# Three expert steps in one loop: the 32-row code moved in front of the 64-row code

## The chip, the cores and the metric

The kernel runs on one core of one Trainium2 chip. The metric is the device time of one execution in microseconds (us); lower is better. The engines are named as the profile names them: PE (matrix multiply, with PEld for its weight loads), DVE (vector), ACT (scalar), POOL (GpSimd), SP (the engine that issues most DMAs). Each engine has a sequencer of its own that reads the engine's instructions, takes its branches and waits on its semaphores.

## The reference

The program normalizes 625 node vectors of 768 numbers, runs a two-layer graph attention network over 20000 edges, adds the result to the input, and then runs a transformer block of 12 attention heads whose feed-forward part is a top-1 mixture of 8 experts. Only that last part bears on this change. Cut to it:

```python
h2 = _ln(x, ln2_g, ln2_b).reshape(-1, d)              # 625 rows of 768
w, sel = jax.lax.top_k(h2 @ Wg, 1)                    # one expert for each row
hid = jax.nn.relu(jnp.einsum('nd,edf->enf', h2, W1) + b1[:, None, :])   # 768 -> 3072
y = jnp.einsum('enf,efd->end', hid, W2) + b2[:, None, :]                # 3072 -> 768
moe = jnp.einsum('ne,end->nd', combine, y)            # each row takes its own expert's y
return x + moe.reshape(b, t, d)
```

W1 and W2 of one expert are 9.4 MB each, in f32.

## The kernel before

Everything ahead of the experts is one straight line of code on every engine (but for one branch at L449 that is there for unusual edge lists). It ends about 700 us into the profiled execution.

**Routing.** The rows are scattered to memory in the order of their experts (`xg` for the layer's input, `xr` for the running sum with the row's number). The expert that the first 125 rows choose most is taken first: one block of 128 of its rows runs ahead of the loop, as straight-line code (`step_a`, L1179). What is left is cut by small vector operations (L1228 to L1306) into blocks of 128, 64 and 32 rows. `table` holds for each block its expert, whether that expert is new, its kind (0 for 128 rows, 1 for 64, 2 for 32) and its first row; `nblk` is their number. Within an expert the order is 32, 64, then all of 128 rows.

**The loop** (L1333) takes one block in each iteration. At its head every engine loads the kind from `table` (L1336), and POOL loads the rows of the next block and the sums of this one. Then one of three versions of the same step runs, chosen by nested conditions on the kind: in memory the code of each engine lies as it is written, the loop's head, the 128-row code, the 64-row code, the 32-row code, the loop's end. The end has the jump back to the head (L1333). A condition that fails is a jump over the code that is not taken; the branch records at L1346 and L1349 are these jumps, and also the jumps from the end of the 128-row and of the 64-row code to the loop's end.

**One step** (`step`, L1075) on M rows: `into(c)` multiplies the rows (`xbT`, turned beforehand) with a piece of W1 into PSUM `ph` (L1091), DVE copies it to `hb` (L1095); `turn(c)` transposes it on PE (`tph`, L1102), and ACT adds the bias and applies the relu into `hbT` (L1107); `out_of(c)` multiplies with a piece of W2 and adds up in PSUM `py` (L1114). Between the last pieces PE turns the rows of the next block (`tpx`, L891). DVE then adds `py` to the sums (`yo`, L1166), and POOL scatters them to the output (L1168). The order of PE's instructions within a step is written out by hand; the three versions do the same work with another split (M=64 and M=32 use groups of the array's columns).

**Weights.** The six pieces of an expert's weights (`ew`, three of W1 and three of W2) have one buffer each. `load_expert` (L1066) issues on SP, within the iteration, the loads of the next block's expert, in twelve DMAs of 1.5 MB and one for `b2b`; each waits until PE has read the piece that it overwrites, and is left out on the chip where the next block's expert is not new.

**Places in PE's code.** Counted from the hint at the loop's head as instruction 0, the built program of before has the first condition at 4, the 128-row code from 6 to 439, the second condition at 441, the 64-row code from 443 to 853, the 32-row code from 855 to 1395, and the jump back to the head at 1399.

Of the kernel before, what the change touches and what calls it, by code (L numbers as in the profile page):

```python
# [62 lines left out]
def gnn_moe_kernel(ctx: ExitStack, tc: tile.TileContext, p, out):  # L63
# [83 lines left out]
    with tc.tile_pool(name="gnn", bufs=1) as gp:  # L147
# [31 lines left out]
        with tc.tile_pool(name="oneh", bufs=12) as op_, \  # L179
# [48 lines left out]
            def step(at, on_act):  # L228
                o = op_.tile([R, SH + 1], F16, name="step")
                if on_act:  # L230
                    nc.scalar.activation(o, iota[:, :SH + 1], AF.Sign, bias=at, scale=-1.0)  # L231
                else:
                    nc.vector.tensor_scalar(o, iota[:, :SH + 1], at, 2.0, op0=OP.is_lt, op1=OP.mult)
                return o
# [821 lines left out]
    def sums_so_far(row):  # L1056
        rb = mw.tile([B, D + 1], F32, name="rb", bufs=1)
        nc.gpsimd.dma_start(rb, xr[ds(row, B), :])
        return rb

    def biases(e):
        bT = mw.tile([128, NK], F32, name="bT")
        of_e = bT_all.rearrange("p (e k) -> p e k", k=NK)[:, ds(e, 1), :]
        return bT, nc.vector.tensor_copy(bT, of_e.rearrange("p o k -> p (o k)"))

    def load_expert(e, new):  # L1066

        with tc.manual_schedule(engines={SP}):
            for l in range(2):
                for c in range(NFC):  # L1070
                    load_piece(e, l, c, cond=new)
                if not l:
                    load_bias(e, cond=new)
# [104 lines left out]
    bT, _ = biases(first_a)  # L1178
# [135 lines left out]
    xbT = ewb.tile([128, KD, B], F32, name="xbT")  # L1314
    row_0 = nc.values_load(table[0:1, 3, 0:1], engines=[pool], min_val=0, max_val=NR - B)
    first_rows = nc.gpsimd.dma_start(xb, xg[ds(row_0, B), :])
    first_turned, = step_a

    def next_expert(i):
        return (nc.values_load(table[0:1, 0, ds(i, 1)], engines=[SP], min_val=0, max_val=E - 1),  # L1320
                nc.values_load(table[0:1, 1, ds(i, 1)], engines=[SP], min_val=0, max_val=1))
# [3 lines left out]
    def all_of(step, e, new):  # L1325
        with tc.manual_schedule(engines={PE}):
            for _ in step:
                pass
        load_expert(e, new)
# [3 lines left out]
    with tc.For_i(0, n_blk, 1, iteration_sync="reg_based") as i:  # L1333
        e = nc.values_load(table[0:1, 0, ds(i, 1)], engines=[mybir.EngineType.DVE], min_val=0,
                           max_val=E - 1)
        kind = nc.values_load(table[0:1, 2, ds(i, 1)], min_val=0, max_val=2)  # L1336
        row, row_next = (nc.values_load(table[0:1, 3, ds(k, 1)], engines=[pool], min_val=0,
                                        max_val=NR - B) for k in (i, i + 1))

        nc.gpsimd.dma_start(xb, xg[ds(row_next, B), :])  # L1340
        rb = sums_so_far(row)
        bT, s = biases(e)
        tc.add_manual_dep(s.ins, first_rows.ins.name, ORDER)

        then = next_expert(i + 1)
        with tc.If(kind == 0) as cmp:  # L1346
            all_of(step(B, xbT, bT, rb, first_turned), *then)
        with cmp.Else():
            with tc.If(kind == 1) as cmp2:  # L1349
                all_of(step(64, xbT, bT, rb, first_turned), *then)  # L1350
            with cmp2.Else():
                all_of(step(32, xbT, bT, rb, first_turned), *then)


# [29 lines left out]
```

## Time and profile before

| | us |
|---|---|
| median of 3 runs (lowest, highest) | 1070.74 (1069.84, 1071.74) |
| the profiled execution's own time | 1070.6 |
| its span, from the first to the last instruction | 1067.9 |
| PE busy in the span | 1006.7 (94%) |
| the loop, first to last matmul | 700.1 to 1055.2 |

The nine iterations in the profiled execution, numbered from 0, by the first matmul of each:

| iteration | 0 | 1 | 2 | 3 | 4 | 5 | 6 | 7 | 8 |
|---|---|---|---|---|---|---|---|---|---|
| rows | 64 | 128 | 64 | 32 | 128 | 64 | 32 | 64 | 32 |
| starts at, us | 700.13 | 736.35 | 801.68 | 840.54 | 866.12 | 931.47 | 965.72 | 993.27 | 1027.52 |

In a line of the timeline, the columns are the start, the time taken, the engine, the line of code, the operation, what it writes and reads, the shapes, how many, and in brackets the idle time before and what ended it. Granted clock is the share of full speed that PE's clock had. The DMA view counts packets by queue; queues of the kind "instruction" bring code to the engines' sequencers.

### The profile page before, as it was taken

To read this page: it belongs to the slowest core of one execution; us is meant where nothing else is said; L and a number is where in the kernel's file an instruction comes from. 1 tells how busy PE (TensorE), PEld (TensorE's weight loads), DVE (VectorE), ACT (ScalarE), POOL (GpSimd) and SP (SyncE) were. 2 spreads that over 40 slices of the span, in tenths; PEclk is the share of its full clock that TensorE was granted. 3 is DMA by queue.
4 is the path that set the end of the run, shared out by engine and by line. 5 is a ranking of instruction groups with operands and counts; after the bars stand their busy time and mean duration, and the time that the engine had idled before them with its cause. 6 is when DMAs were issued, how large, how long until landed. Compare 5 with 4: busy or idle time off the path is not lost. (4 is left out here: it accounts for less than half of the span.)

```text
span 1067.9 us, 14435 instructions
## 1 busy us (share of the span) xinstructions
PE 1006.7 (94%) x4763; PEld 574.8 (54%) x4764; DVE 451.7 (42%) x1264; ACT 319.0 (30%) x817; POOL 57.1 (5%) x97
## 2 busy tenths in 40 slices
PE   6889999999999999999999999999999889998993
PEld 4455465677656556666665654544453435533341
DVE  6886786484284910665438544011101121011211
ACT  6677553452231111444435211110202112021120
POOL 1200100000000100000001101000000000000000
PEclk9999999999999999999999999999999899998997
DMA  9300500301300347998002679012799948899693
GB/s 286 129 1 1 181 9 0 133 1 43 93 14 0 103 120 220 398 389 293 1 2 63 237 251 351 12 46 58 304 321 387 408 177 322 294 413 409 248 412 153
DMA packets 85669, 194.48 MB, mean 182 GB/s; under 512 B 32397, under 2 KB 34068, under 8 KB 85609
## 3 DMA queue, kind: packets, MB, share of 16 engines
q1 hardware_dynamic: 79817, 174.00, 44.3%
q0 software_dynamic: 5712, 19.54, 5.3%
q8 instruction: 36, 0.59, 0.2%
q10 hardware_dynamic: 80, 0.16, 0.1%
q14 instruction: 24, 0.20, 0.1%
HBM read 251.98 MB, written 38.37 MB: 272 GB/s over the span
## 5 line engine op out<-in xcount | busy, mean ns | idle before, releaser
L1114 PE MATMUL py<-ew,hbT 128*64 128x384 f32 (+2 forms) x960 | 196.0, 517 | 12.8 <-DMA ew<-in_L_ffn_W_dram 12.8
L1091 PE MATMUL ph<-ew,xbT 128*32 128x256 f32 (+2 forms) x864 | 153.9, 499 | 7.8 <-issue 4.5
L1114 PEld LDWEIGHTS py<-ew,hbT 128*64 128x64 f32 (+2 forms) x960 | 91.6, 149 | 97.7 <-issue 62.3
L1107 ACT ACTIVATE hbT<-tph,bT 128x64 f32<-128x64 f32 (+2 forms) x240 | 55.3, 333 | 264.2 <-PE tph L1102 162.3
L1091 PEld LDWEIGHTS ph<-ew,xbT 128*32 128x32 f32 (+2 forms) x864 | 63.9, 135 | 87.2 <-issue 79.9
L1166 DVE TENSOR_TENSOR yo<-yo,py 64x384 f32<-64x384 f32 (+2 forms) x40 | 23.0, 608 | 182.9 <-PE py L1114 182.5
L1095 DVE COPY hb<-ph 128x512 f32<-128x512 f32 (+1 forms) x39 | 24.5, 629 | 149.8 <-PE ph L1091 149.8
L528 PE MATMUL agg<-xl,zT 125*125 125x256 f32 (+1 forms) x300 | 79.8, 417 | 1.3 <-ACT zT L517 1.1
L528 PEld LDWEIGHTS agg<-xl,zT 125*125 125x125 f32 x300 | 54.5, 188 | 19.6 <-ACT zT L517 2.6
L231 ACT ACTIVATE step<-iota,past 125x314 f16<-125x314 f16 x120 | 55.9, 548 | 0.0
L356 PE MATMUL pp<-w,yT 128*125 128x512 f32 x120 | 55.3, 600 | 0.0
L628 PE MATMUL ph<-wr,h1T 128*125 128x384 f32 x160 | 52.8, 486 | 0.0
L590 PE MATMUL ph<-w,h1T 128*125 128x384 f32 x160 | 52.4, 486 | 0.0
L837 ACT ACTIVATE e<-e,nm 125x125 f32<-125x125 f32 (+4 forms) x60 | 36.0, 602 | 39.5 <-DVE nm L834 39.5
L248 PE MATMUL cps<-step,oh 125*125 125x314 f16 x181 | 37.4, 309 | 10.5 <-ACT step L231 5.4
L900 PE MATMUL po<-wpj,aT 128*125 128x384 f32 x120 | 44.3, 499 | 1.2 <-DVE nm L834 0.7
L241 DVE TENSOR_SCALAR oh<-iota,drel,upper 125x125 f16<-125x125 f16 x160 | 41.2, 317 | 3.4 <-PE cps L248 3.4
L166 PE MATMUL ph<-wr,yT 128*125 128x512 f32 x96 | 42.1, 593 | 0.1
L590 PEld LDWEIGHTS ph<-w,h1T 128*125 128x125 f32 x160 | 30.0, 188 | 21.2 <-issue 0.5
L628 PEld LDWEIGHTS ph<-wr,h1T 128*125 128x125 f32 x160 | 29.8, 187 | 20.8
L808 PE MATMUL pq<-hT,L_ffn_Wq 128*128 128x313 f32 (+1 forms) x144 | 40.9, 432 | 0.0
L834 DVE CUSTOM_DVE_ANT_0 e<-sc,later 125x125 f32<-125x125 f32 (+4 forms) x60 | 30.7, 544 | 24.1 <-PE sc L828 23.9
(328 smaller groups left out, 1248.9 us busy)
## 6 DMA issues: line engine op xcount, KB each, us to landing
ew<-in_L_ffn_W_dram SPq DMA_DIRECT2D x132, 1536.0 KB
xr<-zt SPq DMA_DIRECT2D x5, 3076.0 KB
xg<-zt SPq DMA_DIRECT2D x5, 3072.0 KB
w<-in_L_gnn_W_dram SPq DMA_DIRECT2D x4, 1536.0 KB
wr<-in_L_gnn_Wr_dram SPq DMA_DIRECT2D x4, 1536.0 KB
b2b<-in_L_ffn_b_dram SPq DMA_DIRECT2D x11, 384.0 KB
xb<-xg POOLq DMA_DIRECT2D x10, 384.0 KB, 6.1
rb<-xr POOLq DMA_DIRECT2D x9, 384.5 KB, 7.0
```

What stands on the lines that cost most here:

```text
L166: nc.tensor.matmul(pp[:R, :], yT[:, c, cols(t)], part(wr1, KD, c, i, 512), start=(c == 0), stop=(c == KD - 1))
L231: nc.scalar.activation(o, iota[:, :SH + 1], AF.Sign, bias=at, scale=-1.0)
L241: m = nc.vector.tensor_scalar(o, iota[:, :n], at, weight, op0=OP.is_equal, op1=OP.mult)
L356: nc.tensor.matmul(pp[:R, :], yT[:, c, cols(t)], part(w1, KD, c, i, 512), start=(c == 0), stop=(c == KD - 1))
L528: nc.tensor.matmul(self.agg[:R, c0:c0 + n], zT[:, s, :], xl[:, s, x0:x0 + n], start=(s == 0), stop=(s == T - 1))
L590: nc.tensor.matmul(ph[:R, :384], h1T[:, c, cols(t)], part(w2, KH, c, i, 384), start=(c == 0), stop=(c == KH - 1))
L628: nc.tensor.matmul(ph[:R, :384], h1T[:, k, cols(t)], part(wr2, KH, k, i, 384), start=(k == 0), stop=(k == KH - 1))
L808: nc.tensor.matmul(pp[:, :b - a], w[:, c, c0:c0 + 128], hT[:, c, a:b], start=(c == 0), stop=(c == KD - 1))
L900: mm = nc.tensor.matmul(pp[:R, i, :384], aT[:, c, cols(t)], wpj[i][:, c, :], start=(c == 0), stop=(c == KD - 1))
L1091: mm = nc.tensor.matmul(ph[g * M:(g + 1) * M, :C], xT[:, k, :M], w[:, k, o + g * C:o + (g + 1) * C], start=(k == 0), stop=(k == KD - 1))
L1107: nc.scalar.activation(hbT[c][:, k, r], tp[:, k, r], AF.Relu, bias=bT[:, f:f + 1])
L1114: mm = nc.tensor.matmul(py[g * M:(g + 1) * M, i, :384], hbT[c][:, k, g * M:(g + 1) * M], w[:, o + g * K + k, i * 384:(i + 1) * 384], start ...
```

## The change

The two versions inside the `Else` change places in memory: the condition is now on kind 2 instead of kind 1, the 32-row code comes first, and the 64-row code last. No instruction of a step changes, and nothing within a step changes its place.

```diff
         then = next_expert(i + 1)
+
         with tc.If(kind == 0) as cmp:
             all_of(step(B, xbT, bT, rb, first_turned), *then)
         with cmp.Else():
-            with tc.If(kind == 1) as cmp2:
+            with tc.If(kind == 2) as cmp2:
+                all_of(step(32, xbT, bT, rb, first_turned), *then)
+            with cmp2.Else():
                 all_of(step(64, xbT, bT, rb, first_turned), *then)
-            with cmp2.Else():
-                all_of(step(32, xbT, bT, rb, first_turned), *then)
```

In PE's code the 32-row code now lies from 443 to 984 and the 64-row code from 986 to 1395; the head, the 128-row code and the loop's end stay where they were. A 64-row step now takes two jumps to its code and none to the loop's end; a 32-row step takes one jump to its code and one to the loop's end. The lines of code below the change are one higher than before (L1346 is L1347, L1349 is L1350).

## The prediction, made before the changed kernel ran

> **What bounds the kernel now.** I read the page first: PE is busy for 94% of the span, so time is lost only where PE waits. The change touches nothing ahead of 700 us, so I then took PE's timeline of the loop, shape by shape, and looked for idle time where iterations meet. Nine iterations meet eight times; only two of these meetings have a gap that no weight load explains.
>
> ```profile
> 729.07 5.38 PE L1114 MATMUL py<-ew,hbT 128*64 128x384 f32 x32
> 736.35 10.54 PE L1091 MATMUL ph<-ew,xbT 128*128 128x512 f32 x24 [1.90 <-DVE yo L1166]
> ...
> 830.61 5.38 PE L1114 MATMUL py<-ew,hbT 128*64 128x384 f32 x32
> 840.54 7.58 PE L1091 MATMUL ph<-ew,xbT 128*32 128x256 f32 x96 [4.55 <-issue]
> ...
> 858.13 0.84 PE L1114 MATMUL py<-ew,hbT 128*32 128x384 f32 x4
> 861.72 4.47 PE L1114 MATMUL py<-ew,hbT 128*32 128x384 f32 x28 [2.75 <-DMA ew<-in_L_ffn_W_dram]
> 866.12 10.57 PE L1091 MATMUL ph<-ew,xbT 128*128 128x512 f32 x24
> ...
> 960.41 5.38 PE L1114 MATMUL py<-ew,hbT 128*64 128x384 f32 x32
> 965.72 5.39 PE L1091 MATMUL ph<-ew,xbT 128*32 128x256 f32 x96
> ...
> 990.56 2.77 PE L1114 MATMUL py<-ew,hbT 128*32 128x384 f32 x28 [1.26 <-DMA ew<-in_L_ffn_W_dram]
> ```
>
> Both gaps follow a 64-row step: 1.90 us after iteration 0 and 4.55 us after iteration 2. The same meeting of 64 and 32 rows after iteration 5 has no gap. The first gap is put down to DVE, but a 64-row step after a 128-row one does not wait for that add; the second is "issue". The reader also sees that the matmuls behind the long gap are slow (7.58 us for 96 against 5.39), and so are the 28 behind the weights (4.47 against 2.77). Third, the windows, for the clock of these stretches:
>
> ```profile
> 835.90:840.50 4.60, 0.10 (x2) 0.00 (x0) 2.22 (x5) 0.00 (x0) 0.95 (x1) 0.74 1.03 412
> 840.50:866.20 25.70, 22.91 (x253) 12.78 (x253) 2.19 (x5) 5.44 (x26) 1.09 (x2) 0.85 0.78 305
> 965.70:993.30 27.60, 22.73 (x256) 9.77 (x254) 4.58 (x10) 5.44 (x26) 2.06 (x3) 0.88 0.88 349
> ```
>
> The last three columns are clock, DMA share and GB/s. The clock was not full; its records in the trace put half speed at 838.08 to 844.91 and 861.98 to 865.39. Fourth, the DMA view of 831 to 837 us and of 866 to 1068 us:
>
> ```profile
> q1 hardware_dynamic: 753, 2.44, 101.0%
> q8 instruction: 1, 0.02, 1.1%
> ...
> q1 hardware_dynamic: 17136, 57.81, 74.2%
> q0 software_dynamic: 1072, 4.78, 6.2%
> ```
>
> In the gap one block of code of 16 KB is fetched; from 866 us on, none. So the gaps are code loading. The trace's branch records on PE give its price. The jump over the 128-row code into iteration 0 (L1346, at 695.67) took 3.69 us; the jump from the end of the 64-row code to the loop's end (L1349) took 3.34 us in iteration 0 (731.08), 5.80 us in iteration 2 (832.62), 0.19 us in iterations 5 and 7. PE's sequencer runs 3 to 4 us ahead of its matmuls, which hides most of a jump of 3.4 us. 5.80 us is the price while the weights stream at 412 GB/s.
>
> **Which code is where.** Between 221.8 and 394.3 us, in straight code, the fetches lie 248 to 259 PE records apart, so a block of 16 KB is taken as 256 instructions. The fetches at 713.22 and 785.35 begin just after the sequencer passes instruction 613 and instruction 357 of the loop, so (an estimate, good to some five instructions) blocks begin at 101, 357, 613, 869, 1125 and 1381: A (the head), B to F, and G (the loop's end). Before, the 64-row code lies in C and D, the 32-row code in D, E, F and G. After, the 32-row code lies in C, D and E, the 64-row code in E, F and G.
>
> The loop's eleven fetches fit one reading. There are at least seven places in a ring. On entering a block, the block that follows is fetched into the next place unless it is there already, whatever that place holds; a missed jump stalls and fills the place after the one in use. By this, iteration 0 leaves C, D and G in places that iterations 1 and 2 overwrite with B, C, D and E, which is why the return to G is missed a second time; from iteration 4 on A to G lie in a row, and nothing is fetched. It is my reading, not a record.
>
> **The change part by part**, against the profiled execution (1070.6 us, 0.14 below the median).
>
> *Entry of iteration 0.* The jump to C stays: 3.69 us, covered by matmuls still running up to 698.78. At 699.41 a second jump now goes to E, which nothing has fetched. Its price: 3.34 us (the jump of iteration 0) less 0.3 us that iteration 0 waits for DVE's adds anyway gives 3.1; 4.4 if it queues behind the 1.24 us fetch of D at 700.07. I take 3.7, near the two rows without traffic. Nothing covers it: the cover was used by the first jump.
>
> *Clock behind it.* PE then idles about 5 us. Gaps of 4.55, 3.10 and 2.75 us were each followed by half clock, and cost 7.58-5.39=2.2, 5.33-2.77=2.6 and 4.47-2.77=1.7 us. I take 2.3; bounds 1.7 and 3.4 (half of the 6.8 us of the longest slow stretch). The page "TensorE: Matmul & The Clock Gate" of the Trainium skill (Part 1) has the clock fall after at least one idle window of about 3.4 us; by it only this gap of 5 us would pay, and the sum below would be about 1.2 smaller, but here 2.75 us was enough.
>
> *End of iteration 0.* The 64-row code runs on into G, already fetched. The gap of 1.90 goes: -1.85 (a meeting without a miss costs 0.05).
>
> *Entry of iteration 2.* In iteration 1, entering B fetches C into E's place (or, if E lies one further, entering C fetches D there), so the jump to E is missed again. It starts at 798.1, 3.6 us before PE runs out. At 3.34 us plus 0.4 to the first matmul it costs 0.1; at 5.80 it costs 2.6, and the clock may then add up to 3.4. E1's last weights run at 319 to 413 GB/s at that time, so the dear row is the nearer, but for a part of the time only, and I take a value between: +2.0, bounds 0.1 and 6.0.
>
> *Iterations 2 and 3.* The 4.55 us gap and the 2.2 us behind it go, but are not won: iteration 3 ends on weights that land about 59.9 us after iteration 2 starts (59.0 for iterations 5 and 7), in the chain of waits:
>
> ```profile
> 836.12 4.87 SPq L1031
> 841.04 0.17 SPq L1031
> 841.44 20.14 DMA ew<-in_L_ffn_W_dram
> 861.72 4.47 PE py L1114 x28
> ```
>
> From landing to the next iteration before: 4.5 us; without slow clock 2.8. Iterations 2 and 3 together took 64.44 us, 5 and 6 61.80, 7 and 8 61.89, so at most 2.6 would be won. But the 32-row code now runs through D and E, each fetched over its neighbour, and entering E fetches F over G. Its jump to the loop's end comes 0.2 us after the landing, misses at 3.5, and 1.8 from there to the first matmul makes 5.5 instead of 4.5: +1.0, less 0.2 for an earlier landing, and about 1.2 for a clock that idles twice: +2.0, bounds -0.2 and +4.5. From iteration 5 on A to G lie in a row again.
>
> *Other engines.* Their branches in the loop took 0.05 to 0.16 us; an extra jump costs DVE 0.1 at the end, and the weight loads that SP issues in iteration 0 move nothing, since the next block's expert is not new (no packet of q1 between 695 and 735 us). Taken as nothing.
>
> Sum: 3.7+2.3-1.85+2.0+2.0 = +8.15; 1070.6+8.15+0.14 = 1078.9.
>
> *A page that speaks against the change more strongly.* "Runtime: NRT & Kernel Launch" (Instruction fetch mechanics) has a window of two pages, and every jump beyond it fetches. By that the 64-row code, now two jumps and more than two pages away, would miss in iterations 5 and 7 too, at an estimated 3 us each more. The row disagrees: 1400 instructions of loop ran from 866 us without one fetch, and far jumps took 0.19 us.
>
> **The rivals.**
> 1. *The return of iteration 3 hits.* If a fetch does not overwrite what is still of use, G stays. Then 2.1 is won there instead of 2.0 lost: 3.7+2.3-1.85+2.0-2.1 = +4.05, 1074.8; with E kept for iteration 2 as well, 1072.8. For it: all seven blocks lie side by side from 866 us on. Against: G was lost between 796 us (a 0.21 us jump to it) and 832.
> 2. *Faster: E comes in the shadow of C.* If the fetch that follows the first miss brought the target of the second jump, iteration 0 would start at most 0.3 us later, and the gains remain: -1.85-2.1+0.3, 1067.1. It decides if the first matmul of the loop is before 701. Against: that fetch (700.07) has fallen on the following block, and E is two further.
> 3. *No difference.* The second jump at 3.1, the clock at 1.7, no later miss, and 2.6 won at iteration 3: +0.4, 1071.
>
> **How the numbers follow.** The forecast 0.62, rival 1 0.27, rival 2 0.04, rival 3 0.07. This kernel's runs can tell about 0.2% (2.1 us) from no change: slower begins at 1072.9, faster at 1068.6. Part of rival 1 lies at that edge (0.02 goes to the same). Faster 0.04, same 0.09, slower 0.87. The forecast's own ends are +2.8 and +16, but four prices do not all fall on one side; together with rival 1 I take 1072.5 to 1083.5.
>
> **What the new profile would show.** Right: a second long branch on PE at about 699.4, the loop's first matmul at 703 to 705, half clock behind it; no gap after iteration 0; a missed jump to E in iteration 2; a missed return, and an idle PE, after iteration 3; nothing fetched from iteration 6 on. Wrong: a first matmul before 701, or a long branch in iterations 5 to 8, or a fetch of instructions there.

## The result and the profile after

Five runs of the changed kernel have a median of 1079.62 us (1077.1 to 1081.87), against 1070.74 before. The medians differ by 8.9 us; the ratio of the runs is put at 1.0076, interval [1.0055, 1.0098]. The forecast was 1078.9. The sum was nearly right, but two of its terms are not in the first profile, and that profile alone would have led to a wrong explanation.

The profiled execution took 1077.1 us, the lowest of its five. Its span is 1074.9 us, 7.0 more than before; all of it lies between the last matmul ahead of the loop and the last one in it (363.53 us against 356.39). PE's timeline of the loop, first the one line of before that shows the entry, then the changed kernel:

```profile
700.13 10.52 PE L1091 MATMUL ph<-ew,xbT 128*64 128x512 f32 x48 [1.35 <-SPq L1333]
```

```profile
694.64 4.03 PE L1114 MATMUL py<-ew,hbT 128*128 128x384 f32 x12
704.28 12.94 PE L1091 MATMUL ph<-ew,xbT 128*64 128x512 f32 x48 [5.61 <-issue]
...
735.63 5.38 PE L1114 MATMUL py<-ew,hbT 128*64 128x384 f32 x32
740.95 10.57 PE L1091 MATMUL ph<-ew,xbT 128*128 128x512 f32 x24
...
806.30 10.52 PE L1091 MATMUL ph<-ew,xbT 128*64 128x512 f32 x48
...
867.58 2.77 PE L1114 MATMUL py<-ew,hbT 128*32 128x384 f32 x28 [2.45 <-DMA ew<-in_L_ffn_W_dram]
870.29 10.57 PE L1091 MATMUL ph<-ew,xbT 128*128 128x512 f32 x24
```

The wait at the entry grew from 1.35 to 5.61 us, and the 48 matmuls behind it took 12.94 us, not 10.52. At 740.95 the gap of 1.90 is gone. At 806.30 and 870.29, where I had missed jumps, there is nothing. The windows of the iterations (us, busy of PE, PEld, DVE, ACT, POOL; then clock, DMA share, GB/s) give the rest; the last line is iterations 5 and 6 of before:

```profile
704.28:740.95 36.67, 36.67 (x187) 14.35 (x187) 2.99 (x5) 6.10 (x26) 1.06 (x2) 0.93 0.07 22
806.30:870.29 63.99, 56.74 (x440) 23.82 (x439) 8.90 (x20) 11.56 (x52) 4.18 (x6) 0.95 0.92 361
935.64:999.95 64.31, 57.03 (x439) 23.87 (x438) 8.90 (x20) 11.57 (x52) 4.19 (x6) 0.95 0.91 360
```

```profile
931.47:993.27 61.80, 56.93 (x440) 23.25 (x439) 8.90 (x20) 11.52 (x52) 4.18 (x6) 0.94 0.95 374
```

Against before: entry +4.26 (5.61 against 1.35), iteration 0 +0.45 (36.67 against 36.22: 2.4 of clock, less the gap of 1.9), iterations 2 and 3 -0.45 (64.44 before), iterations 5 and 6 +2.5 (61.80 before), 7 and 8 +0.35, sum +7.1. Code loading explains the first 4.7 (the entry and iteration 0). In the DMA view of 716 to 1070 us no row of kind "instruction" is left:

```profile
q1 hardware_dynamic: 28560, 96.34, 70.9%
q0 software_dynamic: 1728, 7.82, 5.9%
```

So two theories were open. The **entry theory**: the second jump at the loop's entry is what counts. The **weights theory**: the other order of the code on SP and the other engines lets the weights land later, as iteration 6 suggests.

### The profile page after: what moved, and what is told of

Same layout as the page of the kernel before. It is cut to its first block, busy times and chain, and to the rows that moved or that the text cites. A ratio compares the mean times of both kernels' runs of the same rounds, so it can differ in the third digit from the quotient of the medians.

```text
span 1074.9 us, 14430 instructions
## 1 busy us (share of the span) xinstructions
PE 1010.0 (94%) x4763; PEld 575.0 (53%) x4764; DVE 452.0 (42%) x1264; ACT 319.6 (30%) x817; POOL 57.2 (5%) x97
## 4 chain that ended last, share of the span: by engine, by line
PE 69%; DMA 6%; DVE 6%; issue 4%; ACT 1%; POOL 1%; SPq 0%; DVEq 0%; POOLq 0%; ACTq 0%
PE py L1114 15%; PE ph L1091 15%; PE pq L808 7%; PE agg L528 6%; DMA ew<-in_L_ffn_W_dram 6%; PE ph L590 5%; PE ph L628 3%; PE pv L771 3%; PE ph L166 3%; PE sc L828 2%; PE o L869 2%; PE po L900 2%; PE tpe L851 1%; PE tph L1102 1%; PE tpz L515 1%
## 5 line engine op out<-in xcount | busy, mean ns | idle before, releaser
L1114 PE MATMUL py<-ew,hbT 128*64 128x384 f32 (+2 forms) x960 | 198.2, 515 | 19.9 <-DMA ew<-in_L_ffn_W_dram 19.8
L1091 PEld LDWEIGHTS ph<-ew,xbT 128*32 128x32 f32 (+2 forms) x864 | 60.8, 134 | 88.1 <-issue 79.9
```

What stands on the lines that cost most here:

```text
L1091: mm = nc.tensor.matmul(ph[g * M:(g + 1) * M, :C], xT[:, k, :M], w[:, k, o + g * C:o + (g + 1) * C], start=(k == 0), stop=(k == KD - 1))
L1114: mm = nc.tensor.matmul(py[g * M:(g + 1) * M, i, :384], hbT[c][:, k, g * M:(g + 1) * M], w[:, o + g * K + k, i * 384:(i + 1) * 384], start ...
```

## The experiments

**No weights in the loop.** The line that marks a block's expert as new is taken out of both kernels; no weights are loaded in the loop then, and every block uses the first expert's, so that the outputs are not the program's and only the times are of use. Line numbers behind it are one lower in these two runs.

```diff
-    v.scalar_tensor_tensor(tabf[:, 1, :NS], at, 0.0, u, op0=OP.is_equal, op1=OP.mult)
```

> The order of before (128, 32-row code last), with the flag for a new expert left at zero, so that no weights are loaded in the loop (every block is multiplied with the first expert's weights). What is left is PE and its code. Entry theory (the changed kernel's time is lost on PE's code: a second jump at the loop's entry, 4.15 us, with 2.4 us of half clock behind it, against 1.9 us won after iteration 0): iterations 3, 6 and 8 take 18.1 us each instead of 25.6, 27.5 and 27.6, the missed return after iteration 2 costs about 1.9 instead of 4.6 since no weights delay the fetch, so about 1070.6-29.1=1041.5. Weights theory (the other order makes the weights land later in iterations 3, 6 and 8, and the entry is not what counts): about the same for this kernel; it is the base for the next.

> The changed order (128, 32, 64) with no weights loaded in the loop, as in the run above. Entry theory: first matmul of the loop at 704.3, half clock behind it, no gap after iterations 0 and 2: 4.15+2.4-1.9-1.9 = +2.7 us against the order of before without weights. Weights theory: without weights nothing is left of the loss; the two gaps of before are gone and this order is equal or up to 3.8 us faster.

Measured: 1039.68 us (1038.9 to 1042.94) and 1047.9 us (1044.88 to 1052.13), four runs each. So by the medians most of the loss (8.2 of 8.9 us) is there without weights, and the 2.7 us expected was too little: the run of before lacks the missed return after iteration 2 (0.19 us at 832.98) that was expected to cost 1.9. The timelines, first without the change, then with it:

```profile
700.45 10.52 PE L1091 MATMUL ph<-ew,xbT 128*64 128x512 f32 x48 [1.35 <-SPq L1332]
...
736.72 10.54 PE L1091 MATMUL ph<-ew,xbT 128*128 128x512 f32 x24 [1.95 <-DVE yo L1166]
```

```profile
707.61 11.96 PE L1091 MATMUL ph<-ew,xbT 128*64 128x512 f32 x48 [6.26 <-issue]
...
743.29 10.57 PE L1091 MATMUL ph<-ew,xbT 128*128 128x512 f32 x24
```

The entry costs 4.91 more, iteration 0 0.59 less (half clock, but no gap at its end), and all that follows to the last matmul differs by 0.31 (288.12 against 287.81). In these two profiles the entry and what hangs on it make 4.3 of the 4.6 us that the loop differs by; another 2.3 us lie ahead of the loop, in code that is the same in both. This profile of the changed kernel is among its faster runs; what the runs of 1050 and 1052 us did, no profile shows.

**Other orders of the same code.** 64, 32, 128 rows, and 32, 64, 128 rows (only the first is shown, against the kernel before):

```diff
-        with tc.If(kind == 0) as cmp:
-            all_of(step(B, xbT, bT, rb, first_turned), *then)
+        with tc.If(kind == 1) as cmp:
+            all_of(step(64, xbT, bT, rb, first_turned), *then)
...
-            with tc.If(kind == 1) as cmp2:
-                all_of(step(64, xbT, bT, rb, first_turned), *then)
+            with tc.If(kind == 2) as cmp2:
+                all_of(step(32, xbT, bT, rb, first_turned), *then)
             with cmp2.Else():
-                all_of(step(32, xbT, bT, rb, first_turned), *then)
+                all_of(step(B, xbT, bT, rb, first_turned), *then)
```

> Order 64, 32, 128, with weights. No jump at the loop's entry: 64-row code follows the head. Entry theory: first matmul at 700.1 as before (DVE's adds end at 699.97), one missed jump to the loop's end after iteration 0 (gap 1.9), then at once a missed jump to the 128-row code at instruction 961 with no matmul left to cover it: gap about 5.3 to 6 in all between iterations 0 and 1, with half clock behind it (2.4): 1070.7+3.5+2.4 = 1076.6, range 1074 to 1079. Weights theory: SP reaches the 64-row code sooner than in either kernel, so the weights land earlier: 1069 to 1071.

> Order 32, 64, 128, with weights. One jump at the entry, to the 64-row code at instruction 550, two blocks on: covered as before, first matmul at 700.1. The 64-row code runs through blocks C, D, E; on entering E (91 instructions ahead of its end) F is fetched, so that the jump to the loop's end in G goes to the block after the last one fetched. Entry theory: at most 1.9 us of gap after iteration 0, and nothing fetched later (no hole in what has been fetched, as in the changed kernel): 1070.7 less 0 to 2.6 us at iterations 2 and 3: 1069.5, range 1067.5 to 1071. Weights theory: SP takes as many jumps as in the changed kernel to its 64-row code less one: between the two, 1071 to 1079.

64, 32, 128 took 1079.2 us (1078.09 to 1080.76, ratio 1.0076 [1.0061, 1.009]). Its first iteration falls straight into its code and still waits 1.35 us: that wait is put down to SP at the loop's head and needs no missed jump. The two jumps now queue at the end of iteration 0 (3.20 and 3.63 us in the branch records), with nearly the same gap and the half clock behind it. A third missed jump, the return of iteration 3 (3.73 us at 869.49), left another gap of 3.31 us, which I had not expected; it helps to put the time above the 1074 to 1079 that I gave:

```profile
701.06 10.52 PE L1091 MATMUL ph<-ew,xbT 128*64 128x512 f32 x48 [1.35 <-SPq L1333]
...
740.91 13.59 PE L1091 MATMUL ph<-ew,xbT 128*128 128x512 f32 x24 [5.53 <-issue]
...
875.46 12.24 PE L1091 MATMUL ph<-ew,xbT 128*128 128x512 f32 x24 [3.31 <-DVE yo L1166]
```

32, 64, 128 had a median of 1079.19, but its twelve runs lie apart: three at 1068.3 to 1068.5, two at 1072 to 1074, seven at 1079 to 1082. Its first profile was one of the low ones. The order of the code alone doesn't fix the time; something differs from one execution to the next.

**One jump instead of two, and further profiles.** The steps lie in memory as in the changed kernel, but both tests stand ahead of the 128-row code, so that PE reaches the 64-row code by one jump (the diff is against the changed kernel):

```diff
-        with tc.If(kind == 0) as cmp:
-            all_of(step(B, xbT, bT, rb, first_turned), *then)
-        with cmp.Else():
-            with tc.If(kind == 2) as cmp2:
-                all_of(step(32, xbT, bT, rb, first_turned), *then)
-            with cmp2.Else():
-                all_of(step(64, xbT, bT, rb, first_turned), *then)
+        with tc.If(kind != 2) as cmp:
+            with tc.If(kind == 0) as cmp2:
+                all_of(step(B, xbT, bT, rb, first_turned), *then)
+            with cmp2.Else():
+                all_of(step(64, xbT, bT, rb, first_turned), *then)
+        with cmp.Else():
+            all_of(step(32, xbT, bT, rb, first_turned), *then)
```

> The code of the steps lies as in the changed kernel, 128, 32, 64 rows, and the 64-row code runs on into the loop's end; but both tests of the kind stand ahead of the 128-row code, so that TensorE reaches the 64-row code by one jump instead of two. Entry theory: one missed jump (3.3 to 3.7 us in all traces) ends about 699.3, where the matmuls in hand still hide most of it, so the gap at the loop's entry is 1.35 us instead of 5.61, no half clock follows (2.42 us), and iteration 0 ends without a gap as in the changed kernel: 1079.6 - 4.26 - 2.42 = 1072.9, and with it 1.9 under the kernel before less what the weights take (1068.8 if nothing): 1068 to 1074. Weights theory (it is the order of the code on SP and the other engines that lets the weights land later, and the entry is not what counts): 1077 to 1080, with the entry at 1.35 us all the same.

> The changed kernel once more, one profile. Entry theory: the gap at the entry is again 5 to 6 us with half clock behind it, and the waits for weights in iterations 3, 6 and 8 differ from the first profile by what one execution differs from the next (up to 3 us each way), 1077 to 1082. Weights theory: iteration 6 waits 7.2 us again, as in the first profile, against 4.9 in the kernel before.

> The kernel before once more, one profile. Entry theory: 1069 to 1074, gap at the entry 1.35 us, 1.9 us after iteration 0; the waits for weights in iterations 3, 6 and 8 may differ by up to 3 us from the first profile. Weights theory: iteration 6 waits 4.9 us again and iterations 5 and 6 take 61.8 us, not 64.3.

> Order 32, 64, 128 rows once more: its times lay at 1068.4 and at 1079 to 1082, and the first profile was one of the low ones, with nothing fetched after 732 us. If this is a high one (about 1079): by the entry theory it shows further missed jumps or fetches after iteration 0, by the weights theory none, and longer waits for weights, 10 us in all. If a low one again: the same picture as the first.

As written, this code has the 64-row version second, but in memory it is not laid out as it is written. The trace has the 64-row code last: a 64-row step ends without a jump (iteration 0, before the return to the head at 731.98), a 32-row step with one (861.63).

With one jump: 1078.97 us (1077.07 to 1080.52), ratio 1.0069 [1.005, 1.0089]. The entry did what the entry theory says, and the time did not:

```profile
700.79 10.52 PE L1091 MATMUL ph<-ew,xbT 128*64 128x512 f32 x48 [1.34 <-SPq L1333]
...
735.04 10.57 PE L1091 MATMUL ph<-ew,xbT 128*128 128x512 f32 x24
...
803.34 10.52 PE L1091 MATMUL ph<-ew,xbT 128*64 128x512 f32 x48 [2.88 <-DVE bT L1064]
...
841.62 7.07 PE L1091 MATMUL ph<-ew,xbT 128*32 128x256 f32 x96 [3.97 <-DMA ew<-in_L_ffn_W_dram]
...
1037.98 8.25 PE L1091 MATMUL ph<-ew,xbT 128*32 128x256 f32 x96 [3.86 <-issue]
```

The entry gap is back at 1.34 us, with no half clock and no gap after iteration 0; but from the entry of iteration 2 on (796.66) there are missed jumps of 3.5 to 6.3 us, still at 1031.97 (5.74 us in the branch record), and 16 fetches of 16 KB between 716 and 1070 us. (The releasers in the brackets are inferred; here the branch records and the fetches tell the cause.) What was saved up to the end of iteration 0, 6.7 us against the changed kernel, came back as refetches. As I read it, the direct jump left out the blocks between the head and the 64-row code; the fetches at 750.1 and 784.3, while iteration 1 runs through the 128-row code, bring two of them, and from then on blocks still needed were missing. The trace does not say which block a fetch brings or overwrites. So the entry theory holds for the entry and fails for the time.

The second profile of the changed kernel, 1081.11 us, shows what the forecast had and the first profile had not:

```profile
704.51 12.37 PE L1091 MATMUL ph<-ew,xbT 128*64 128x512 f32 x48 [5.45 <-issue]
...
808.82 10.52 PE L1091 MATMUL ph<-ew,xbT 128*64 128x512 f32 x48 [2.80 <-DVE bT L1064]
...
873.76 13.11 PE L1091 MATMUL ph<-ew,xbT 128*128 128x512 f32 x24 [4.08 <-DVE yo L1166]
```

and its DMA view of 716 to 875 us has eight fetches of code:

```profile
q1 hardware_dynamic: 11424, 38.54, 63.8%
q0 software_dynamic: 656, 3.04, 5.5%
q8 instruction: 8, 0.13, 0.4%
```

The jump to the 64-row code misses in iteration 2 (802.37, 6.07 us), the return to the loop's end misses after iteration 3 (867.13, 4.86 us), and the clock falls behind it (13.11 us for 24 matmuls against 10.57). Against the first profile the loop is 4.2 us longer: iteration 1 +2.9, iteration 3 +0.95, iteration 4 +2.55, iteration 6 -1.7, the rest -0.5. Iterations 5 and 6 took 62.6 us here, against 64.3: of the 2.5 us on which the weights theory stood, 1.7 vary from one execution to the next.

The second profile of the kernel before (1069.5 us) lacks the missed jump of 5.80 us at 832.62, and with it the 4.55 us gap. It gains almost nothing: iterations 2 and 3 took 63.87 us instead of 64.44, since PE then waits for the weights instead. These also came later in this execution: the last wait for them in iteration 3 ended 61.17 us after iteration 2 began, 60.04 in the first profile. The branch records show a difference between two executions of one program. At the first return to the loop's head the jump back (L1333) took 0.25 to 0.27 us where no fetch followed, and 0.37 or 0.38 us where a block was fetched 1.0 to 1.2 us after it began: before (first profile), the changed kernel (second) and 32, 64, 128 (second profile, 1083.15 us). In that last run three missed jumps followed each other from 732.04 us on (3.50, 4.45 and 4.91 us):

```profile
746.89 12.35 PE L1091 MATMUL ph<-ew,xbT 128*128 128x512 f32 x24 [11.47 <-issue]
```

Against its low run the loop took 14.0 us more; this gap and the slow clock behind it are 11.0 of them.

**Fewer blocks.** PE's part of the loop starts at a block of 256 instructions, in both kernels; the loop then lies in 6 blocks instead of 7. The order 64, 128, 32 ran beside them.

```diff
-    with tc.For_i(0, n_blk, 1, iteration_sync="reg_based") as i:
+    with tc.For_i(0, n_blk, 1, iteration_sync="reg_based", head_align_engines=(PE,)) as i:
```

> The changed kernel with TensorE's part of the loop starting where a code block of 256 instructions starts, so that the loop lies in 6 blocks instead of 7. The second test then lies in the loop's second block, which is fetched with the first, and only the jump on to the 64-row code (4th block) can miss at the entry. Entry theory: gap at the entry 1.35 to 2.2 us instead of 5.61, no half clock behind it, no gap after iteration 0: 1079.6 - 3.4 to 4.3 - 2.4 = 1073 to 1074, and 1069 to 1071 if with one block fewer nothing is fetched again later. Skipped-block theory (a block that the first iteration jumped over, here the third, is fetched later over one that is still needed, as in the kernel with one jump): entry as said, but fetches and missed jumps from iteration 1 on, 1076 to 1081.

> The kernel before with the same alignment. Entry theory: gap at the entry 1.35 us as before (64-row code in the second block, fetched with the first), 1.9 us or a little more after iteration 0, where the code jumps over the fifth block to the loop's end: 1069 to 1072. Skipped-block theory: the fifth block is fetched in iteration 3, where it may cost what the waits for the weights do not cover: 1069 to 1075.

> Order 64, 128, 32 rows: the first iteration falls straight into its code, its end jumps over both other codes to the loop's end (one missed jump, 1.9 us as before), and the 128-row code follows in blocks that are fetched already. Entry theory: gap at the entry 1.35 us as before, since that gap is there without a missed jump too; the same as before, 1069 to 1072. Skipped-block theory: the jump leaves out two to three blocks that are fetched later; 1070 to 1079, with missed jumps in iterations 1 to 3.

Twelve runs each: the changed kernel aligned 1074.97 us (1072.85 to 1077.68), 4.65 less than without alignment (an earlier set of runs) and still 1.0023 [1.0007, 1.004] of the kernel before; the kernel before aligned 1069.26 us (1068.33 to 1074.26), ratio 0.9982 [0.9966, 0.9997], a little faster than both kernels; 64, 128, 32 rows 1070.91 us, no difference (0.9989 [0.9974, 1.0004]): its first pass has no jump at the entry and a gap of 2.24 us at the end of iteration 0, and the jump that misses in iteration 1 (3.68 us at 799.06) is hidden. The aligned pair's timelines, the changed kernel first:

```profile
704.12 12.77 PE L1091 MATMUL ph<-ew,xbT 128*64 128x512 f32 x48 [4.96 <-issue]
...
740.62 10.57 PE L1091 MATMUL ph<-ew,xbT 128*128 128x512 f32 x24
...
805.97 10.52 PE L1091 MATMUL ph<-ew,xbT 128*64 128x512 f32 x48
```

```profile
700.48 10.52 PE L1091 MATMUL ph<-ew,xbT 128*64 128x512 f32 x48 [1.35 <-SPq L1333]
...
736.59 10.54 PE L1091 MATMUL ph<-ew,xbT 128*128 128x512 f32 x24 [1.79 <-DVE yo L1166]
```

I expected the second jump alone to miss at the entry; both did (2.45 and 5.05 us). The first one's fetch began at 696.08, 0.09 us ahead of the jump; I take it that the loop's second block is fetched only when the first is entered. Both profiles have no fetch of code for PE between 738 us and the last matmul. So the aligned pair shows the entry by itself: +3.6 of gap and +0.4 in iteration 0, and 0 to 0.3 in each part up to iteration 6; iterations 7 and 8 are 3.1 us longer in the changed kernel, in waits for weights. The medians differ by 5.7 us, and with 7 blocks by 8.9.

**One jump and fewer blocks.** Both edits together.

> The kernel with one jump to the 64-row code (code in the order 128, 32, 64, both tests ahead), with TensorE's part of the loop starting at a code block, in 6 blocks. Room theory (later misses come because 7 blocks do not all stay; 6 stay whatever the order in which they were fetched): entry 1.35 us, no half clock, no gap after iteration 0, blocks left out at the entry fetched once in iteration 1 without loss; 1.8 us under the aligned kernel before, 1066 to 1069, below both kernels. Skipped-block theory (a block left out at the entry is fetched later over one still needed, however many there are): entry as said, but fetches and missed jumps in most iterations, as with one jump and 7 blocks, 1074 to 1081.

Measured: 1072.03 us (1070.72 to 1074.79), ratio 1.0001 [0.9987, 1.0015]: between the two expectations.

```profile
700.66 10.52 PE L1091 MATMUL ph<-ew,xbT 128*64 128x512 f32 x48 [1.63 <-SPq L1333]
...
734.90 10.57 PE L1091 MATMUL ph<-ew,xbT 128*128 128x512 f32 x24
...
803.33 12.22 PE L1091 MATMUL ph<-ew,xbT 128*64 128x512 f32 x48 [3.00 <-DVE bT L1064]
```

The entry and iteration 0 are as cheap as hoped (iteration 0: 34.24 us against 36.11 in the aligned kernel before), then the left-out blocks cost three missed jumps (6.50, 4.63, 3.20 us at 796.4, 837.4, 862.5), and nothing from iteration 4 on. With 7 blocks the misses went on to the last iteration. So both seem to count: a block jumped over is paid for later, and with one block less the loop recovers.

## Why the prediction was right, and where it was not

- **Second jump at the entry, +3.7.** Right: it began at 699.21 (forecast 699.41) and the gap grew by 4.26 and, in the second profile, 4.10, inside the bounds and near their upper end (3.1 plus 1.24 makes that end 4.3, not 4.4). The jump took 4.69 us; its fetch ran beside another, by its place the one of the block that follows the first target: 2.25 us from 700.28, while that one began at 699.87. Where a second jump's fetch ran alone, in 64, 32, 128 rows, it took 1.06 us and the jump 3.63.
- **Half clock, +2.3.** Right: 2.4 and 1.85 us on the 48 matmuls. In the aligned kernel and in 64, 32, 128 rows, gaps of 4.96 and 5.53 us were followed by 2.25 and 3.05 us of the same loss.
- **End of iteration 0, -1.85.** Right: the gap of 1.90 is gone in every order that runs on into the loop's end.
- **Entry of iteration 2, +2.0, and return of iteration 3, +2.0.** The step that failed is the one ahead of both: that the blocks overwrite each other in every execution. In the first profile neither jump missed: for the code, that is rival 1 with E kept. The 2.1 us that this rival would win at iteration 3 shrank to 0.45, since the last weights there ended their wait 61.28 us after iteration 2 began, against 60.04 before. In the second both missed, at +2.9 and, over iterations 2 to 4, +3.05 against before (64.94-64.44, and 67.90-65.35). My reading of the ring had one course; the runs show at least two for one program. That the median came within 1 us of the sum is in part luck: the first profile lacks both terms and has 2.9 us in iterations 5 to 8 that the sum put at nothing, the second has both terms at more than was forecast, and what the run of the median did, no profile shows.
- **Where a refetch falls decides its price.** In before the profile with the missed jump lost only 0.6 us to the one without, because that jump lies inside a stretch that ends on weights (had the weights landed alike, it would have been an estimated 1.7 us, from 60.04 and 61.17); in the changed kernel one miss lies at the end of a 128-row iteration and the other after the last weights of iteration 3, where nothing covers them. The forecast had this for iterations 2 and 3, and it held where the jumps missed.
- **Weights, taken as nothing.** Not foreseen as an unsteady term: iterations 5 and 6 took 61.8 us in both profiles of before, 64.3 and 62.6 after, 63.2 and 63.6 in the aligned pair. It makes 2.5 us of the first profile's +7. That it has nothing to do with the order is not shown: iterations 5 to 8, free of missed jumps, took 126.6, 125.1 and (aligned) 127.5 us in the three profiles of the changed order, 123.7, 123.6 and (aligned) 124.1 in the three of before, and 123.1 to 125.6 in the other orders, but for one jump with 7 blocks, where jumps miss. Without weights these iterations differ by 0.3 us only. So in these few profiles 1 to 4 us lie in the arrival of the weights, by a cause that stays open. The weights theory is refuted as the whole cause, by the kernels without weights, but not as a part of it.
- **Rivals 2 and 3** fall. Against rival 2, the first matmul of the loop came at 704.3 and 704.5, not before 701. Against rival 3, the gap at the entry grew by 4.26 and 4.10 us instead of 3.1, and iterations 2 and 3 won 0.45 or nothing instead of 2.6. The two-page window that I weighed does not describe this loop: in the first profile the whole loop ran from 716 us on without a fetch.

Left open: why, at the first return to the loop's head, the block behind the head is gone in some executions and there in others, with the same fetches up to then. The trace records fetches, not what is kept.

## What to carry to other kernels

Where a loop's code is many blocks long, add up the jumps of its first pass. Here one missed jump of 3 to 4 us was hidden by the matmuls in hand, wholly or but for some 2 us; a second one queued behind it was paid nearly in full, and half clock followed the idle time. A jump that skips blocks which later code runs through can move the price instead of saving it, so count the blocks left out as well. Starting the loop at a block's beginning helped both orders here, by 4.65 and 2.25 us of the medians. And take a second profile before explaining a gap: here the loop of one program took 4.2 us more in the second profile than in the first.

## What the runs showed of the hardware

- The wait of 1.35 us at the loop's entry stays when no jump misses there (64, 32, 128 rows), so the missed jump of 3.69 us in front of it in the kernel before costs nothing.
- One program, two courses: the jump back took 0.25 to 0.27 us, or 0.37 to 0.38 with a block fetched behind it; what followed cost between 0.6 us (before) and some 11 us (32, 64, 128 rows).
- Two queued missed jumps gave 4.96 to 6.26 us of idle PE wherever they lay; three in a row gave 11.5 us.
- In 6 blocks the loop had no fetch after iteration 0 in both original orders, one profile each. In 7 blocks it went on fetching up to iteration 3 in both profiles of before and in the second of the changed kernel, but not in the first. So the blocks may be the reason, but they don't decide it alone.
